# Silu moved to other units, and one 1024-element scan in place of two 512-element scans in 14 of 24 units of a Mamba kernel

## Chip, cores and metric

The kernel runs on one core of a Trainium2 chip. The metric is the device time of one execution in microseconds (us). The kernel before takes 11815.42 us, the median of 3 runs (11808.57 to 11817.72).

## What is computed

Two layers work on an image x of 2 x 96 x 128 x 128 (batch, channels, height, width). Layer 0 adds a four-direction Mamba block to x, then a feed-forward block in 8-bit floats; layer 1 adds a 3x3 convolution and a second feed-forward block. Each has a normalisation ahead of it. The change is inside the Mamba block. For each direction, with L = 16384 positions, 192 inner channels and 16 states:

```
xc = silu(conv1d(in-projection of x)); z = the other half of the projection
dt = softplus(dt_raw @ dt_w.T + dt_b)
dA[t] = exp(dt[t] * A)                      per channel and state
h[t]  = dA[t] * h[t-1] + dt[t] * B[t] * xc[t]
y[t]  = sum over states of h[t] * C[t]  +  D * xc[t]
out   = (y * silu(z)) @ outp_w.T
```

The recurrence in h is the part that can't be cut into independent pieces: it is a scan along t.

## The kernel before

For each of the two images the kernel normalises, runs the Mamba part, and then runs a fused stage of both feed-forward blocks and the convolution. The Mamba part takes the four directions in two pairs. A pair's 2 x 192 channels fill three groups (g = 0, 1, 2) of 128 partitions. A **step** is one block of T = 512 positions of one pair; there are 64 steps for an image and 128 in all. A **unit** is one group and two neighbouring states, so a step has 3 x 8 = 24 units, numbered u = 0 to 23 (k counts them across steps). For a unit:

- ACT (ScalarE) writes dA for both states to a PSUM tile `da` of 128 x 2 x 512 with two Exp instructions (`decay`, L364). The pool has three such tiles, and the loop asks for unit k+2 while unit k is scanned.
- POOL (GpSimd) multiplies the broadcast rows of B by dt*xc in place (`b_part`, L354), four states, that is two units, at a time, and adds the carried-in state to the first column of each state (L358), after one product for a group's start (L357). So a scan may start from 0.
- DVE (VectorE) runs the scan of each state (`scan`, L368), in place in `da`, and then multiplies both states by C (L456, in `behind`). In three units of a step (u = 4, 8, 10; the list BY_POOL) the scan writes into the B tile instead, and POOL does the product (L375).
- ACT copies the last column of h to `hst` (L457), and PE (TensorE) sums the products over states into one PSUM tile `y` (L372). At the end of a group DVE multiplies y by silu(z) (`gated`, L379).

Every engine's order is the order in which the Python code issues. [...] The main loop, for each k, issues this: the steps queued for (k, 0); the scan of the first state; `behind(k-1)`, that is the product, the copy to hst and the sums of the unit before; `decay(k+2)`; the scan of the second state; and the steps queued for (k, 1). On even k `b_part` of units k+2 and k+3 goes ahead of all that. On DVE, this puts the product of unit k-1 between the two scans of unit k.

While one step is scanned, the preparation of the next (or of the one after: its position list runs past 24 into the following step) is issued in small parts, from the list `at` in `prologue`: (position, 0 or 1 for the two places in a unit, function). ACT's parts are `conv_out` (L241), `gate_out` (L249), `rows_out` (L274), `dt_exp` (three instructions, L291 to L294), `dt_ln` (three, L299 to L302), `entry` (L320), `collect` (L393, L395), and `silu` (L261, L262): a load of another function table, one Silu over 128 x 1536, and the load of the usual table. POOL's parts are `dt_q` (L305), `dt_log` (L308), `dt_sum` (L311) and `dt_u` (L315). The small tiles e, q and ln between ACT and POOL have one buffer each, so ACT's `dt_exp` of one group waits for POOL's `dt_q` of the group before. PE's parts (`conv`, `gate`, `rows`, `dt_in`, `project`) all go through one PSUM bank, `misc`. SP issues the broadcasts of B and C rows from DRAM (`row_tile`, `fetch`), the re-sorting of xc and sz (`mix`), and the rows' way to DRAM.

Of the kernel before, what the change touches and what calls it, by code (L numbers as in the profile page):

```python
# [14 lines left out]
AF = mybir.ActivationFunctionType  # L15
ALU = mybir.AluOpType
# [17 lines left out]
C_AHEAD = 2  # L34
AHEAD = 2
BY_POOL = ((0, 8), (1, 0), (1, 4))
BCO = 32
NBC = 4 * S

# [2 lines left out]
def tile_metaformer(ctx: ExitStack, tc: tile.TileContext, a: dict, out: bass.AP):  # L42
    nc = tc.nc
# [5 lines left out]
    def const(name, shape):  # L49
        t = cpool.tile(list(shape), F32, name=name)  # L50
        nc.sync.dma_start(t, a[name])
        return t
# [7 lines left out]
    minus_one = cpool.tile([128, 1], F32, name="minus_one")  # L60
# [14 lines left out]
    convb = const("convb", (128, 2, NG))  # L75
    bcw = const("bcw", (128, 2, NG, BCO + NBC))
    dtw = const("dtw", (2 * RK, 2, NG * 128))
# [5 lines left out]
    amat = cpool.tile([128, 2, NG, S], F32, name="amat")  # L83
# [103 lines left out]
    def mamba(acc, xnr, xnc):  # L187

        with ExitStack() as st:
# [26 lines left out]
            def prologue(pi, i, d):  # L216

                rev = pi == 1
                lo = L - (i + 1) * T if rev else i * T
# [44 lines left out]
                def rows():  # L264

                    d["ps"] = misc()
                    for g in range(NG):
                        nc.tensor.matmul(  # L268
                            d["ps"][0 : BCO + NBC, :], bcw[:, pi, g, :], d["xc"][:, g, :], start=g == 0, stop=g == NG - 1
                        )  # L270

                def rows_out():
                    d["rows"] = one.tile([BCO + NBC, T], F32, name="rows")
                    nc.scalar.copy(d["rows"], d["ps"][0 : BCO + NBC, :])  # L274

                def rows_to_dram():

                    d["bcd"] = rows_d.tile([2, S // 4, 2, 4, T], F32, name="bcd")
                    nc.sync.dma_start(d["bcd"].rearrange("k q d s t -> (k q d s) t"), d["rows"][BCO:, :])

# [41 lines left out]


                first = pi == 0 and i == 0
                at = [(-3, 1, load), (3, 0, partial(mix, "xc")), (11, 0, partial(silu, "xc"))]
                at += [(9, 0, partial(mix, "sz")), (31, 1, partial(silu, "sz"))]
                at += [(12, 0, rows), (13, 1, rows_out), (14, 0, rows_to_dram)]
                for g, k in ((1, 1), (0, 5), (2, 9)):
                    at += [(k, 0, partial(conv, g)), (k + 1, 1, partial(conv_out, g))]
                for g, k in ((1, 7), (0, 17), (2, 21)):  # L330
                    at += [(k, 0, partial(gate, g)), (k + 1, 0, partial(gate_out, g))]
                dts = ((24, 25, 26, 27), (31, 32, 33, 35)) if first else ((18, 19, 20, 22), (22, 23, 24, 26))
                for g, ks in enumerate(((14, 15, 16, 18), *dts)):
                    at += [(k, 0, partial(f, g)) for k, f in zip(ks, (dt_in, dt_exp, dt_ln))]
                    at += [(ks[3] - 1, 1, partial(dt_q, g))]
                    at += [(ks[3] + m, 0, partial(f, g)) for m, f in ((1, dt_log), (1, dt_sum), (2, dt_u))]
                    if i > 0:
                        at += [((20, 24, 29)[g], 1, partial(entry, g))]

                outs = (conv_out, gate_out, rows_out, dt_exp)  # L340
                at = [(k, where, getattr(f, "func", f) not in outs, f) for k, where, f in at]
# [18 lines left out]
            def decay(pi, d, g, s):  # L360

                da = ps_w.tile([128, 2, T], F32, name="da")
                for j in range(2):
                    nc.scalar.activation(da[:, j, :], d["dt"][g], AF.Exp, scale=amat[:, pi, g, s + j : s + j + 1])  # L364
                return da

            def scan(j, da, b, h):
                nc.vector.tensor_tensor_scan(h[:, j, :], da[:, j, :], b[:, j, :], 0.0, ALU.mult, ALU.add)  # L368

            def sums(s, y, c):  # L370
                for j in range(2):
# [27 lines left out]
            units = [(g, s) for g in range(NG) for s in range(0, S, 2)]  # L399
            nu = len(units)  # L400
            total = nu * len(steps)
# [3 lines left out]
            def later(k, where, rank, f, *args):  # L405
                todo.setdefault((k, where), []).append((rank, partial(f, *args)))

            def issue(k, where):
                for _, f in sorted(todo.pop((k, where), ()), key=lambda p: p[0]):
                    f()  # L410

            for k, where, rank, f in prologue(*steps[0], state[0]):
                if k < nu:
                    f()
                else:
                    later(k - nu, where, rank, f)

            def prepare(n):
                if n < len(steps):
                    for m, where, rank, f in prologue(*steps[n], state[n]):  # L420
                        k = (n - 1) * nu + m
                        if k < 0:
                            f()
                        else:
                            later(k, where, rank, f)

            prepare(1)
            bs, cs, das, hs, quads = {}, {}, {}, {}, {}

            def fetch(k, n, ahead, m):  # L430
                if k < total:
                    t = row_tile(state[k // nu], *units[k % nu], n, ahead)
                    m[k], m[k + 1] = t[:, 0:2, :], t[:, 2:4, :]
                    if n == 0:
                        quads[k] = t

            def feed(k):

                if k < total:
                    n = k // nu  # L440
                    b_part(steps[n][1], state[n], *units[k % nu], quads.pop(k))

            def feed_decay(k):
                if k < total:
                    n = k // nu
                    das[k] = decay(steps[n][0], state[n], *units[k % nu])
# [3 lines left out]
            def behind(k):  # L450

                n, u = divmod(k, nu)
                (pi, i), d, (g, s) = steps[n], state[n], units[u]
                h, c = hs.pop(k), cs.pop(k)
                if (g, s) not in BY_POOL:
                    nc.vector.tensor_tensor(c, h, c, ALU.mult)  # L456
                nc.scalar.copy(hst[:, g, s : s + 2], h[:, :, T - 1])  # L457
                if s == 0:
                    if k > 0:
                        pn, pu = divmod(k - 1, nu)  # L460
                        gated(steps[pn][0], state[pn], units[pu][0], ys.pop(k - 1))
                    y = ps_y.tile([128, T], F32, name="y")
                    nc.tensor.matmul(y, dmat[:, pi, g, :], d["xc"][:, g, :], start=True, stop=False)  # L463
                else:
                    y = ys.pop(k - 1)
                ys[k] = y
                if (g, s) in BY_POOL:
                    later(k + 1, 1, True, by_pool, h, c)
                    later(k + 3, 1, True, sums, s, y, c)
                else:  # L470
                    sums(s, y, c)
                if k == total - 1:
                    gated(pi, d, g, y)
                if s == S - 2 and g > 0:
                    later(k + 4, 0, True, project, pi, i, d, g)
                    later(k + 5, 1, False, collect, pi, d, g)
# [7 lines left out]
            for k in range(total + 6):  # L484
                n, u = divmod(k, nu)
                if u == nu - 3:

                    prepare(n + 2)
                if k % 2 == 0:
                    fetch(k + 2 * B_AHEAD, 0, B_AHEAD, bs)  # L490
                    feed(k + AHEAD)
                issue(k, 0)
                if k < total:
                    (g, s) = units[u]
                    da, b = das.pop(k), bs.pop(k)
                    hs[k] = b if (g, s) in BY_POOL else da
                    scan(0, da, b, hs[k])
                if 0 < k <= total:
                    behind(k - 1)
                feed_decay(k + AHEAD)  # L500
                if k < total:
                    scan(1, da, b, hs[k])
                if k % 2 == 0:
                    fetch(k + 2 * C_AHEAD, 1, C_AHEAD, cs)
                issue(k, 1)
# [101 lines left out]
    for b in range(NB):  # L607
        xnr = dpool.tile([C, L], F32, name="xnr")
        xnc = dpool.tile([C, L], F32, name="xnc")
        normalize(b, acc, xnr, xnc)  # L610
        mamba(acc, xnr, xnc)
        ffn_and_conv(b, acc)


def _layout(v):
# [9 lines left out]
    xw = v["L0_conv_xproj_w"]  # L625
    bcw = np.zeros((2, 2 * DI, BCO + NBC), f)
    dtw = np.zeros((2 * RK, 2, 2 * DI), f)
# [56 lines left out]
```

## Time and profile before

| what | value |
|---|---|
| median of 3 runs | 11815.42 us |
| the profiled execution: its own time | 11813.3 us |
| its span | 11811.5 us |
| busy in the span: DVE | 10818.5 us, 92% |
| PE | 10510.1 us, 89% |
| POOL | 10203.6 us, 86% |
| ACT | 8548.6 us, 72% |
| granted TensorE clock | 0.99 |
| step of the Mamba part: nine Silu of `sz`, from 2927.8 to 3577.1 us, so 649.3 us for 8 steps | 81.16 us |

A span is cut into the 40 slices of the page's second part: the two Mamba parts take about 18 slices each, with the busy DVE, POOL and DMA; the slices with POOL at 1 are the fused stage. In the timeline an instruction's line gives its start, its duration, engine, source line and operation, then the number merged into the line (x2), and, in brackets, how long the engine stood idle ahead of it and what released it. Neighbours on one engine overlap a little: a scan lasts 1.21 us, but the next instruction starts 1.12 us after it did. For sums, the distance from start to start is therefore used, and it is called the pitch.

### The profile page before, as it was taken

The page shows a single profiled execution, that of the slowest core. Times are in us where ns is not written, and L with a number is a line of the kernel's source. Part 1 is how long each engine was busy: PE and PEld are TensorE (multiplying, and loading weights), DVE is VectorE, ACT ScalarE, POOL GpSimd, SP SyncE. Part 2 cuts the span into 40 slices and gives each one's busy share as a digit, 9 for nine tenths or more (in the row PEclk, how much of TensorE's full clock was granted, in tenths as well). Part 3 has the DMA queues.
Part 4 walks back from the last instruction along what each step waited for, and adds up shares of the span by engine and source line. Part 5 has one row for each costly group of instructions (what it writes and reads, how often), then busy time and mean ns, then how long its engine had stood idle before and what let it go on. Part 6 is the DMA issues. An engine that isn't in the chain of part 4 may idle for free. (4 is left out here: it accounts for less than half of the span.)

```text
span 11811.5 us, 96408 instructions
## 1 busy us (share of the span) xinstructions
PE 10510.1 (89%) x24208; PEld 3894.5 (33%) x24208; DVE 10818.5 (92%) x10512; ACT 8548.6 (72%) x15094; POOL 10203.6 (86%) x5468
## 2 busy tenths in 40 slices
PE   7888888989888889889978888888898898888899
PEld 2333333333333333333323333333333333333333
DVE  6999999999999999994469999999999999999944
ACT  6777777777777777775567777777777777777755
POOL 5999999999999999991159999999999999999911
PEclk9999999999999999999989999999999999999999
DMA  7888888888888888880068888888888888888800
GB/s 263 323 323 324 321 327 321 320 330 318 327 324 323 324 324 321 327 317 24 26 242 319 327 324 322 324 325 320 328 320 323 328 318 327 324 323 323 319 14 13
DMA packets 540774, 3417.11 MB, mean 289 GB/s; under 512 B 67532, under 2 KB 68652, under 8 KB 143832
## 3 DMA queue, kind: packets, MB, share of 16 engines
q1 hardware_dynamic: 539960, 3410.16, 75.6%
q8 instruction: 195, 3.19, 0.1%
q14 instruction: 363, 2.97, 0.1%
q0 software_dynamic: 256, 0.79, 0.0%
HBM read 3289.04 MB, written 54.53 MB: 283 GB/s over the span
## 5 line engine op out<-in xcount | busy, mean ns | idle before, releaser
L354 POOL TENSOR_TENSOR row<-dtu,row 128x2048 f32<-128x2048 f32 x1536 | 6957.6, 4530 | 11.4 <-DMA row<-bcd 8.7
L368 DVE TENSOR_TENSOR_SCAN da<-da,row 128x512 f32<-128x512 f32 x5376 | 6324.3, 1213 | 208.0 <-ACT da L364 127.7
L372 PE MATMUL y<-row,ident 128*128 128x512 f32 x12288 | 5778.2, 604 | 667.5 <-DVE row L456 643.5
L364 ACT ACTIVATE da<-dt,amat 128x512 f32<-128x512 f32 x6144 | 4249.0, 692 | 184.3 <-POOL dt L311 1.7
L372 PEld LDWEIGHTS y<-row,ident 128*128 128x128 f32 x12288 | 2231.1, 190 | 4058.8 <-issue 2155.2
L456 DVE TENSOR_TENSOR row<-da,row 128x1024 f32<-128x1024 f32 x2688 | 3233.6, 1203 | 0.1
L457 ACT COPY hst<-da 128x2 f32<-128x2 f32 x2688 | 423.6, 158 | 2400.8 <-DVE row L456 2380.7
L213 PE MATMUL misc<-xb,inx 96*64 96x512 f32 (+1 forms) x2048 | 956.5, 610 | 130.8 <-ACT hst L457 110.4
L579 POOL TENSOR_TENSOR acc<-acc,y 96x512 f32<-96x512 f32 x128 | 147.6, 1153 | 993.9 <-DVE y L578 993.9
L368 DVE TENSOR_TENSOR_SCAN row<-da,row 128x512 f32<-128x512 f32 x768 | 927.3, 1207 | 50.6 <-ACT da L364 44.8
L213 PE MATMUL misc<-xa,inx 96*64 96x512 f32 (+1 forms) x2048 | 940.8, 602 | 27.0 <-DMA xa<-xnr 17.3
L375 POOL TENSOR_TENSOR row<-row,row 128x1024 f32<-128x1024 f32 x384 | 904.0, 2354 | 18.0 <-DVE row L368 17.1
L305 POOL TENSOR_TENSOR q<-e,q 128x512 f32<-128x512 f32 x384 | 488.5, 1272 | 261.3 <-ACT hst L457 173.4
L591 PE MATMUL pc<-pad,kw 96*96 96x512 f32 x1152 | 567.0, 593 | 0.0
L463 PE MATMUL y<-xc,dmat 128*128 128x512 f32 x768 | 421.3, 630 | 149.9 <-DVE sz L379 149.9
L311 POOL TENSOR_TENSOR dt<-dt,ln 128x512 f32<-128x512 f32 x384 | 488.6, 1272 | 30.1
L213 PEld LDWEIGHTS misc<-xa,inx 96*64 96x64 f32 (+1 forms) x2048 | 314.5, 163 | 604.2 <-issue 426.0
L315 POOL TENSOR_TENSOR dtu<-dt,xc 128x512 f32<-128x512 f32 x384 | 488.6, 1272 | 0.5
L308 POOL TENSOR_TENSOR ln<-ln,q 128x512 f32<-128x512 f32 x384 | 487.5, 1270 | 0.2
L389 PE MATMUL misc<-sz,gmat 128*96 128x512 f32 x1024 | 483.6, 594 | 0.0
L268 PE MATMUL misc<-xc,bcw 128*96 128x512 f32 x768 | 364.4, 611 | 117.6 <-ACT xc L261 91.9
L213 PEld LDWEIGHTS misc<-xb,inx 96*64 96x64 f32 (+1 forms) x2048 | 316.9, 164 | 434.1 <-issue 204.0
(82 smaller groups left out, 8926.2 us busy)
## 6 DMA issues: line engine op xcount, KB each, us to landing
row<-bcd SPq DMA_DIRECT2D x3072, 1024.0 KB, 6.4
xc<-mix SPq DMA_DIRECT2D x256, 128.0 KB, 5.4
sz<-mix SPq DMA_DIRECT2D x256, 128.0 KB, 8.4
xa<-xnr SPq DMA_DIRECT2D x124, 193.1 KB, 5.2
xb<-xnc SPq DMA_DIRECT2D x124, 193.1 KB, 5.4
bcd<-rows SPq DMA_DIRECT2D x128, 128.0 KB, 6.9
acc<-in_x_dram SPq DMA_DIRECT2D x16, 768.0 KB, 5.9
xnr<-xn SPq DMA_DIRECT2D x16, 768.0 KB, 4.3
```

The costliest lines, as they stand in the source:

```text
L213: nc.tensor.matmul(ps[rows, :], w(PAIRS[pi][d], k, lo, hi), src[d][:, k : k + T], **se)
L305: nc.gpsimd.tensor_tensor(d["q"], d["e", g], d["q"], ALU.subtract)
L308: nc.gpsimd.tensor_tensor(d["ln"], d["ln"], d["q"], ALU.add)
L311: nc.gpsimd.tensor_tensor(d["dt"][g], d["dt"][g], d["ln"], ALU.add)
L315: nc.gpsimd.tensor_tensor(dtu, d["dt"][g], d["xc"][:, g, :], ALU.mult)
L354: nc.gpsimd.tensor_tensor(b, d["dtu"][g][:, None, :].broadcast_to((128, 4, T)), b, ALU.mult)
L364: nc.scalar.activation(da[:, j, :], d["dt"][g], AF.Exp, scale=amat[:, pi, g, s + j : s + j + 1])
L368: nc.vector.tensor_tensor_scan(h[:, j, :], da[:, j, :], b[:, j, :], 0.0, ALU.mult, ALU.add)
L372: nc.tensor.matmul(y, ident, c[:, j, :], start=False, stop=s + j == S - 1)
L375: nc.gpsimd.tensor_tensor(c, h, c, ALU.mult)
L456: nc.vector.tensor_tensor(c, h, c, ALU.mult)
L591: nc.tensor.matmul(pc, kw[:, t, :], rows, start=t == 0, stop=t == 8)
```

## The change

```diff
+SPLIT = (4, 5, 10, 11, 15, 16, 18, 19, 22, 23)
...
-                at = [(-3, 1, load), (3, 0, partial(mix, "xc")), (11, 0, partial(silu, "xc"))]
-                at += [(9, 0, partial(mix, "sz")), (31, 1, partial(silu, "sz"))]
-                at += [(12, 0, rows), (13, 1, rows_out), (14, 0, rows_to_dram)]
+                at = [(-3, 1, load), (3, 0, partial(mix, "xc")), (11, 1, partial(silu, "xc"))]
+                at += [(9, 0, partial(mix, "sz")), (29, 1, partial(silu, "sz"))]
+                at += [(13, 0, rows), (14, 1, rows_out), (15, 0, rows_to_dram)]
...
-                dts = ((24, 25, 26, 27), (31, 32, 33, 35)) if first else ((18, 19, 20, 22), (22, 23, 24, 26))
-                for g, ks in enumerate(((14, 15, 16, 18), *dts)):
+                dts = ((24, 25, 26, 27), (32, 33, 34, 35)) if first else ((18, 19, 20, 22), (22, 23, 24, 26))
+                for g, ks in enumerate(((15, 16, 17, 18), *dts)):
                     at += [(k, 0, partial(f, g)) for k, f in zip(ks, (dt_in, dt_exp, dt_ln))]
-                    at += [(ks[3] - 1, 1, partial(dt_q, g))]
+                    at += [(ks[3], 1, partial(dt_q, g))]
                     at += [(ks[3] + m, 0, partial(f, g)) for m, f in ((1, dt_log), (1, dt_sum), (2, dt_u))]
...
                 da = ps_w.tile([128, 2, T], F32, name="da")
+                part = units.index((g, s)) not in SPLIT
+                if part:
+                    nc.scalar.activation(da[:, 1, 0:1], minus_one, AF.Copy, scale=0.0)
                 for j in range(2):
-                    nc.scalar.activation(da[:, j, :], d["dt"][g], AF.Exp, scale=amat[:, pi, g, s + j : s + j + 1])
+                    lo = j if part else 0
+                    scale = amat[:, pi, g, s + j : s + j + 1]
+                    nc.scalar.activation(da[:, j, lo:], d["dt"][g][:, lo:], AF.Exp, scale=scale)
                 return da

             def scan(j, da, b, h):
-                nc.vector.tensor_tensor_scan(h[:, j, :], da[:, j, :], b[:, j, :], 0.0, ALU.mult, ALU.add)
+                da, b, h = (t[:, j, :] if j is not None else t.rearrange("p j t -> p (j t)") for t in (da, b, h))
+                nc.vector.tensor_tensor_scan(h, da, b, 0.0, ALU.mult, ALU.add)
...
-                    scan(0, da, b, hs[k])
+                    scan(0 if u in SPLIT else None, da, b, hs[k])
                 if 0 < k <= total:
                     behind(k - 1)
                 feed_decay(k + AHEAD)
-                if k < total:
+                if k < total and u in SPLIT:
                     scan(1, da, b, hs[k])
```

In 14 units of a step, called joined units below, one scan runs over both states' 1024 elements. The zero that ACT writes at the first column of the second state's dA cuts the chain there: 0 * h + b is b, which holds the carried-in state. The Exp of the second state then covers 511 elements. The joined scan stands where the first scan stood, and the product of the unit before comes after it instead of between two scans. The 10 units of SPLIT keep their two scans.

The Silu of xc goes from (11, 0) to (11, 1), behind `decay(13)`. The Silu of sz goes from (31, 1) to (29, 1), that is from u = 7 to u = 5 of the following step, ahead of `entry` of group 2. The rows' product, copy and store move one unit later, as do `dt_in`, `dt_exp` and `dt_ln` of group 0. For every group POOL's `dt_q` moves from the end of one unit to the end of the next, so that the `b_part` of two units, which stood between `dt_q` and `dt_log`, now comes ahead of both.

## Prediction

> **What bounds the kernel now.** I read four views in this order: busy time by engine, with one stretch inside the Mamba part; the groups of instructions; who waited for whom; then the timeline of one step, engine by engine. First the busy times, and the stretch from 2000 to 3000 us (columns: its length, then PE, PEld, DVE, ACT, POOL, clock, DMA share, GB/s):
>
> ```profile
> PE 10510.1 (89%) x24208; PEld 3894.5 (33%) x24208; DVE 10818.5 (92%) x10512; ACT 8548.6 (72%) x15094; POOL 10203.6 (86%) x5468
> ```
>
> ```profile
> 2000.00:3000.00 1000.00, 894.99 (x2049) 330.02 (x2048) 981.77 (x888) 748.71 (x1327) 965.61 (x508) 1.00 0.85 323
> ```
>
> In the Mamba part DVE is busy 98% and POOL 97%: two engines near their limit. Who waits, with total and number of times:
>
> ```profile
> POOL q L305 <- ACT hst L457: 173.4, 126, 3.0
> DVE da L368 <- ACT da L364: 127.7, 126, 1.0
> DVE row L368 <- ACT da L364: 44.8, 112, 0.4
> ```
>
> DVE stalls only behind ACT, twice a step (172.5 us in all); it never waits for POOL in the steady state. POOL waits once a step, 1.38 us, at the first `dt_q`. So DVE with its two stalls sets the step of 81.16 us, and POOL follows with 1.4 us to spare. The stalls, on DVE and on ACT:
>
> ```profile
> 3012.17 1.22 DVE L368 TENSOR_TENSOR_SCAN da<-da,row 128x512 f32<-128x512 f32 x1
> 3013.80 1.22 DVE L368 TENSOR_TENSOR_SCAN row<-da,row 128x512 f32<-128x512 f32 x1 [0.41 <-ACT da L364]
> ...
> 3021.81 1.22 DVE L368 TENSOR_TENSOR_SCAN da<-da,row 128x512 f32<-128x512 f32 x1
> 3024.03 1.23 DVE L368 TENSOR_TENSOR_SCAN da<-da,row 128x512 f32<-128x512 f32 x1 [1.01 <-ACT da L364]
> 3043.72 2.33 DVE L368 TENSOR_TENSOR_SCAN da<-da,row 128x512 f32<-128x512 f32 x2
> 3045.96 1.20 DVE L456 TENSOR_TENSOR row<-da,row 128x1024 f32<-128x1024 f32 x1
> ```
>
> ```profile
> 3018.40 1.28 ACT L261 ACT_TABLE_LOAD   x1
> 3019.70 1.48 ACT L261 ACTIVATE xc<-xc 128x1536 f32<-128x1536 f32 x1
> 3021.20 1.28 ACT L262 ACT_TABLE_LOAD   x1
> 3022.49 0.19 ACT L457 COPY hst<-row 128x2 f32<-128x2 f32 x1
> 3022.59 1.41 ACT L364 ACTIVATE da<-dt,amat 128x512 f32<-128x512 f32 x2
> ```
>
> Each stall ends with the second Exp behind a Silu burst (3018.40 to 3022.49: 4.09 us). The last two DVE lines give pitches: two scans 2.24, so 1.12 each; a product also 1.12; the gated product (3039.76 to 3040.35) 0.59. A step's DVE work is 48 x 1.12 + 21 x 1.12 + 3 x 0.59 = 79.05, plus 0.13 at each of three places where both scans of a unit stand together (3.49 for three scans, where 3.36 would do): 79.4. With the stalls and 0.1 of lost overlap at each, 79.4 + 1.62 = 81.1, against 81.16 measured.
>
> POOL's pitches:
>
> ```profile
> 3035.17 0.20 POOL L358 TENSOR_TENSOR row<-row,enter 128x4 f32<-128x4 f32 x1
> 3036.80 1.28 POOL L305 TENSOR_TENSOR q<-e,q 128x512 f32<-128x512 f32 x1 [1.42 <-ACT hst L457]
> 3038.02 4.53 POOL L354 TENSOR_TENSOR row<-dtu,row 128x2048 f32<-128x2048 f32 x1
> 3042.63 0.20 POOL L358 TENSOR_TENSOR row<-row,enter 128x4 f32<-128x4 f32 x1
> 3042.78 1.27 POOL L308 TENSOR_TENSOR ln<-ln,q 128x512 f32<-128x512 f32 x1
> 3044.13 1.27 POOL L311 TENSOR_TENSOR dt<-dt,ln 128x512 f32<-128x512 f32 x1
> 3045.36 4.54 POOL L354 TENSOR_TENSOR row<-dtu,row 128x2048 f32<-128x2048 f32 x1
> ```
>
> A quad with its edge takes 4.76 (3038.02 to 3042.78), 4.95 with L357, L375 2.31. A 512-element operation takes 1.23 if the next needs nothing of it, 1.35 if the next reads its result (ln to dt). Sum: 9 x 4.76 + 3 x 4.95 + 3 x 2.31 + 3 x (1.23 + 1.35 + 1.23 + 1.24) = 79.77; with the wait of 1.4 it is 81.17.
>
> [...]
>
> **The change, part by part.**
>
> *The joined scan.* From gated (512: 0.59) and product (1024: 1.12), the fixed part of an instruction is 0.06; the scan then streams 512 in 1.06. A scan of 1024 has pitch 2 x 1.06 + 0.06 = 2.18 to 2.19, and saves about 0.055. No row shows one: below, nothing excludes 2.13 (no fixed part at all)[...]. I take 2.185. DVE per step: 20 x 1.12 + 14 x 2.185 + 21 x 1.12 + 1.77 + 0.26 (the joined unit 9 drops one of the three places) = 78.54. This is 0.9 less than 79.4.
>
> *ACT's extra copy.* Between 0.09 (overlapped) and 0.29 (the 128x16 ACTIVATE L320); I take 0.2. It lengthens each joined unit's turn on ACT (hst, copy, two Exps) from 1.55 to 1.75, and 1.81 to the end of the second Exp.
>
> *Slack.* The Exps of unit k+2 may start once the product of k-1 has ended. Before, they end 2.8 us ahead of their scan (3045.4 against 3048.2). In joined rows, with the product behind the long scan, they start 3.4 us after the start of unit k and have to be done at 6.6: 6.6 - 3.4 - 1.8 = 1.4 left. The dt work fits: in units 16 to 24 ACT carries 1.82 (`dt_exp`) or 1.93 (`dt_ln`) beside 1.6 to 1.75 in a unit of 3.3 to 3.9, and a backlog of 0.1 to 0.4 never reaches 1.4.
>
> *Silu of sz.* Time 0 is the start of unit 4. DVE: unit 5 at 3.36, unit 6 at 5.73 (two scans, no product: unit 4's is POOL's), unit 7 at 9.04, unit 8 at 12.35; product 5 ends at 9.12. ACT: hst and Exps for unit 6 from 2.35 to 4.10; collect 1.05, to 5.15; hst and Exps for 7 (no product to wait for) 1.6, to 6.75; Silu to 10.84; `entry` 0.29, to 11.1; hst and Exps for 8 end at 12.93. Unit 8 starts 0.6 late, 0.7 with the overlap.
>
> *Silu of xc.* Time 0 is unit 10. Exps for 12 end at 4.10, `conv_out` at 4.77, Exps for 13 at 6.37, Silu at 10.46, Exps for 14 at 12.27; unit 14 starts at 12.35. No stall. Its two users follow: the rows, now at unit 13, and `dt_in` at 15 keep their one-unit distances. So DVE and ACT alone would give 78.54 + 0.7 = 79.25, and DVE would no longer be last.
>
> *POOL.* What is late next is POOL. Its wait of 1.4 goes, but `dt_log` now reads q directly behind `dt_q` (1.35 instead of 1.23, three times), and for one group `b_part` directly follows the `dt_u` that it reads (once more): 79.77 + 4 x 0.12 = 80.25. This is its floor with no wait. The bounds are 79.77 (the waits cost nothing) and 80.25 plus whatever makes it wait. With POOL last, the first `dt_q` comes behind one more quad (4.73) while ACT's `dt_ln` comes one unit (3.3) later, so the wait is covered by 1.4. The tightest of its other waits, the product of unit 10, has about 0.7 to spare.
>
> *Queues.* rows to DRAM move from 14 to 15; the first fetch that reads them is issued at 18, three units or 10 us later; the store lands in 6.9 us. The cover is 3 us here, and a further four units until `b_part` uses the rows. PE's 72.6 us a step stay. The first step's shifted `dt` costs nothing that repeats.
>
> *Sum.* 81.16 to 80.25 is 0.91 a step; over 126 steps in the steady state, 115 us. Against the profiled execution's 11813.3 (span 11811.5 plus 1.8) this is 11698; the median, 2 us higher, gives 11700.
>
> **Rivals.**
>
> 1. *POOL bound at 80.25* (forecast): 11700. For it: 97% busy, contiguous but for one wait. Against: only 0.9 us above DVE's own sum. Spread 11670 to 11725.
> 2. *The added POOL waits cost nothing*, or overlap as before: floor 79.77, 1.39 x 126 = 175, 11640 (11615 to 11665).
> 3. *ACT is tied to POOL*: `dt_exp` of group 2 waits for `dt_q` of group 1 (e has one buffer), which moved a unit later. On POOL it ends 49.6 us after the quad of unit 8; ACT wants it at 50.3. With POOL late by 1 us, ACT takes this over, and with 2.9 more DVE does. A mixed cycle of about 80.75: 0.41 x 126 = 52, 11763 (11735 to 11790).
> 4. *Slower: PE late ahead of the Silu bursts.* `collect` and `conv_out` stand directly ahead of Silu on ACT and wait for PE, 89% busy. [...] each us of delay there reaches units 8 and 14 in full, since the slack is gone. Against: now such waits are short (ACT waited 21.1 us on `conv_out` in all). It decides from 81.3 - 79.25 = 2.1 us a step. With 1.25 us at each place, 81.75: +74, 11890.
> 5. *No effect*: joined scans cost as much as two, and POOL keeps waiting elsewhere: 11815.
>
> **How the numbers follow.** Chances: forecast 0.58, second 0.14, third 0.14, slower 0.10, none 0.04. 0.2% (24 us) is about what a measurement of this kernel can tell from no change. Faster by more than that: 0.58 + 0.14 + 0.11 of the third = 0.83, rounded to 0.82; within: 0.03 + 0.04 = 0.07; slower 0.11. The range 11625 to 11780 holds the forecast, most of the second and most of the third, 0.58 + 0.12 + 0.11 = 0.81.
>
> **What would show it.** A 1024-element scan with a pitch near 2.19; a 128x1 ACT copy near 0.2; the wait POOL q <- ACT gone; DVE waiting for POOL's rows (L354, L358) about 1 us a step, mostly at units 8, 12 and 14, and for ACT at unit 8 at most; POOL near 98% in the Mamba part; a step of 80.25. The prediction is wrong if POOL still waits, if the scan's pitch is above 2.24, or if ACT's waits on PE ahead of Silu grow.

## The result, and the profile after

The changed kernel takes 12003.11 us (median of 4 runs, 11998.69 to 12006.19) against 11812.17 for the kernel before in the same comparison: a ratio of 1.0161, 95% interval 1.0143 to 1.0179. It is slower, where a gain of 1% was forecast. In the profiled execution the span is 12004.4 us, and a step, from the Silu of xc at 2908.6 us to the eighth after it at 3571.0, is 662.4 / 8 = 82.80 us instead of 81.16.

First the busy times by engine, then a stretch of 1000 us in the Mamba part (columns as before: length, PE, PEld, DVE, ACT, POOL, clock, DMA share, GB/s):

```profile
PE 10618.6 (88%) x24208; PEld 3978.5 (33%) x24208; DVE 10738.7 (89%) x8720; ACT 8845.1 (74%) x16886; POOL 10219.6 (85%) x5468
```

```profile
2000.00:3000.00 1000.00, 891.68 (x1998) 334.06 (x1997) 951.56 (x698) 759.82 (x1463) 944.18 (x492) 0.97 0.83 316
```

DVE has fallen from 98% to 95%, but POOL, which was to go to 98%, is at 94%. Neither of the two is the limit all the time: each waits for a chain that contains the other. Who waited for whom (total, times, longest):

```profile
POOL row L355 <- DMA row<-bcd: 290.3, 119, 6.1
ACT e L292 <- POOL q L306: 282.4, 165, 3.3
DVE da L378 <- POOL row L359: 224.6, 247, 2.2
DVE row L378 <- POOL row L359: 217.0, 124, 1.8
```

DVE now waits for POOL, as forecast, but 3.5 us a step (441.6 in all) and not about 1. POOL's wait at q is gone: 1.1 us where 173.4 were. In its place POOL waits 290 us, 2.3 a step, for B rows to arrive from DRAM, where the kernel before lost 8.7 us in all. Here is POOL's timeline around one such wait, which is for the rows of units 20 and 21:

```profile
3002.13 4.52 POOL L355 TENSOR_TENSOR row<-dtu,row 128x2048 f32<-128x2048 f32 x1
3006.72 0.21 POOL L359 TENSOR_TENSOR row<-row,enter 128x4 f32<-128x4 f32 x1
3010.97 4.53 POOL L355 TENSOR_TENSOR row<-dtu,row 128x2048 f32<-128x2048 f32 x1 [4.04 <-DMA row<-bcd]
3015.57 0.20 POOL L359 TENSOR_TENSOR row<-row,enter 128x4 f32<-128x4 f32 x1
3015.72 1.28 POOL L306 TENSOR_TENSOR q<-e,q 128x512 f32<-128x512 f32 x1
3017.08 1.27 POOL L309 TENSOR_TENSOR ln<-ln,q 128x512 f32<-128x512 f32 x1
```

The same moment in SP's queue (start, duration, number of fetches), and on PE:

```profile
2991.61 1.23 SPq L351 DMA_DIRECT2D row<-bcd  x2
3003.43 0.80 SPq L351 DMA_DIRECT2D row<-bcd  x2
3005.14 0.32 SPq L351 DMA_DIRECT2D row<-bcd  x1
```

```profile
2993.71 3.48 PE L382 MATMUL y<-row,ident 128*128 128x512 f32 x4 [2.13 <-DVE row L466]
2996.98 2.98 PE L269 MATMUL misc<-xc,bcw 128*96 128x512 f32 x6
2999.80 5.31 PE L382 MATMUL y<-row,ident 128*128 128x512 f32 x12
```

SP issues fetches strictly in turn: B of 16, C of 14, B of 18, C of 16, B of 20, C of 18. From 2992.8 to 3003.43, for 10.6 us, it issues none. The first of the two fetches at 3003.43 is that of C rows for units 16 and 17. It needs the buffer of units 10 and 11, and unit 10 is one of POOL's: its sums on PE are issued three units later, at the end of unit 13. On PE these are the second four matmuls of the line at 2999.80 (four make a unit of two states: the page counts 12288 on this line for 3072 units), so they end near 3003.4, and SP moves at once. The B rows of unit 20 stood behind in the queue. Their own buffer had been free for 7 us (its last scan, unit 13's, ended at 2995.9), and they land 7 us after they are issued, when POOL has been idle for 4. A part of the delay is PE's speed: the line at 2993.71 took 3.48 us for four matmuls, where 1.88 is usual (the last section comes back to this).

The same place in the kernel before, PE and SP:

```profile
3023.89 1.88 PE L372 MATMUL y<-row,ident 128*128 128x512 f32 x4
3026.44 3.70 PE L372 MATMUL y<-row,ident 128*128 128x512 f32 x8 [0.67 <-DVE row L456]
```

```profile
3030.17 0.80 SPq L350 DMA_DIRECT2D row<-bcd  x2
```

There too SP stood in C rows until unit 10's sums ended at 3030.1. But that was 6.1 us after the start of unit 13 (3024.03), and after the change it is 9.9 (3003.43 against 2993.57). And there POOL waited at q for ACT in the meantime, did q, and came to those rows at 3038.02, when they had landed. The trace of before hardly shows a wait for DMA (8.7 us), because another wait lay over it; run 15 tests this.

### The profile page after: what moved, and what is told of

It is laid out like the page before. It is cut to its first block, busy times and chain, and to the rows that moved or that the text cites. A ratio compares the mean times of both kernels' runs of the same rounds, so it can differ in the third digit from the quotient of the medians.

```text
span 12004.4 us, 96788 instructions
## 1 busy us (share of the span) xinstructions
PE 10618.6 (88%) x24208; PEld 3978.5 (33%) x24208; DVE 10738.7 (89%) x8720; ACT 8845.1 (74%) x16886; POOL 10219.6 (85%) x5468
## 3 DMA queue, kind: packets, MB, share of 16 engines
q1 hardware_dynamic: 539960, 3410.16, 74.4%
## 5 line engine op out<-in xcount | busy, mean ns | idle before, releaser
L382 PE MATMUL y<-row,ident 128*128 128x512 f32 x12288 | 5908.1, 617 | 822.2 <-DVE row L466 820.2
L378 DVE TENSOR_TENSOR_SCAN da<-da,row 128x512 f32<-128x512 f32 (+1 forms) x3712 | 6209.3, 1695 | 333.2 <-POOL row L359 224.6
L372 ACT ACTIVATE da<-dt,amat 128x512 f32<-128x512 f32 (+1 forms) x6144 | 4247.7, 691 | 192.9 <-POOL dt L312 1.6
L378 DVE TENSOR_TENSOR_SCAN row<-da,row 128x512 f32<-128x512 f32 (+1 forms) x640 | 913.3, 1427 | 222.4 <-POOL row L359 217.0
L214 PE MATMUL misc<-xa,inx 96*64 96x512 f32 (+1 forms) x2048 | 970.8, 617 | 28.1 <-DMA xa<-xnr 17.6
L214 PE MATMUL misc<-xb,inx 96*64 96x512 f32 (+1 forms) x2048 | 974.4, 620 | 18.7 <-ACT mix L250 13.5
L292 ACT ACTIVATE e<-misc,dtb 128x512 f32<-128x512 f32 x384 | 262.2, 683 | 407.5 <-POOL q L306 282.4
L214 PEld LDWEIGHTS misc<-xa,inx 96*64 96x64 f32 (+1 forms) x2048 | 332.8, 168 | 643.7 <-issue 490.3
L287 PE MATMUL misc<-rows,dtw 12*128 12x512 f32 x768 | 439.2, 651 | 11.1 <-ACT sz L250 9.4
```

The source lines that it names most:

```text
L214: nc.tensor.matmul(ps[rows, :], w(PAIRS[pi][d], k, lo, hi), src[d][:, k : k + T], **se)
L372: nc.scalar.activation(da[:, j, lo:], d["dt"][g][:, lo:], AF.Exp, scale=scale)
L378: nc.vector.tensor_tensor_scan(h, da, b, 0.0, ALU.mult, ALU.add)
L382: nc.tensor.matmul(y, ident, c[:, j, :], start=False, stop=s + j == S - 1)
```

## The experiments

Each run is compared with the kernel before, measured beside it (medians of 11809.48 to 11813.75 us). Ratios carry their 95% intervals; "step" is the mean distance of seven or eight Silu of xc near 3000 us.

**1. One more buffer for C rows.**

```diff
-                t = gen.tile([128, 4, T], F32, name=f"row{k}", bufs=ahead + 1)
+                t = gen.tile([128, 4, T], F32, name=f"row{k}", bufs=ahead + 1 + k)
```

(Also `io` with 1 buffer and dt, dtu with 3, for the space.)

> Theory (the queue): in the changed kernel POOL is last, as forecast at 80.25 us a step, but loses a further 2.3 us because SP, which issues all row fetches in order, stands in a fetch of C rows until PE has done the sums of unit 10, and the B rows of unit 20 are queued behind it. A fourth buffer for C rows takes that wait away: POOL's wait for B rows falls from 290 us to under 60, the step to about 80.4, the time to 11720 (11690 to 11760). Rival (the transfers): the rows come late because the DMA engines are short of throughput (median landing 7.1 us against 6.4); then nothing is gained, 11950 to 12010. Two other pools are made smaller to hold the buffer (xa and xb single, three buffers for dt and dtu); each theory expects nothing of that.

Measured: 11840.81 us, 1.0026 (1.0016 to 1.0037). POOL's wait for B rows is 6.4 us in all. So the queue is shown, and throughput is refuted: nothing was taken off the DMA engines, whose main queue moved 3410.16 MB in both kernels. But the time stayed 120 us above the expectation. Two waits that were small in the changed kernel (7.6 and 1.1 us) have come up:

```profile
DVE sz L389 <- PE y L382: 203.7, 128, 3.1
POOL q L306 <- ACT hst L467: 138.2, 90, 3.1
```

**2. B rows first.**

```diff
                 if k % 2 == 0:
                     fetch(k + 2 * B_AHEAD, 0, B_AHEAD, bs)
+                    if k > 0:
+                        fetch(k + 2 * C_AHEAD - 2, 1, C_AHEAD, cs)
...
-                if k % 2 == 0:
-                    fetch(k + 2 * C_AHEAD, 1, C_AHEAD, cs)
```

> The changed kernel with each fetch of C rows issued two units later, behind the fetch of B rows of that moment, and no other edit. Theory (the queue): SP no longer holds B rows back; POOL's wait for B rows nearly goes, 11700 to 11780, unless the C rows now come late for the product (a wait of DVE L466 on a DMA would show it). Rival (the transfers): about 12000, with the wait unchanged.

Measured: 11839.81 us, 1.0025 (1.0015 to 1.0035). POOL's wait for B rows is gone, so this agrees with the first run by another way. C rows come late by 4.7 us in all for DVE's products and by 26.1 for POOL's. The same wait on PE appears: once a step, 1.4 to 1.6 us, ahead of the gated product of unit 9. The timelines of PE, ACT and DVE in this run show its cause:

```profile
3013.34 0.64 PE L214 MATMUL misc<-xa,inz 96*64 96x512 f32 x1 [0.78 <-ACT hst L467]
...
3014.34 5.42 PE L382 MATMUL y<-row,ident 128*128 128x512 f32 x12
```

```profile
3009.38 1.28 ACT L263 ACT_TABLE_LOAD   x1
...
3012.61 0.67 ACT L242 ACTIVATE xc<-misc,convb 128x512 f32<-128x512 f32 x1
```

```profile
3019.80 0.69 DVE L389 TENSOR_TENSOR sz<-y,sz 128x512 f32<-128x512 f32 x1 [1.38 <-PE y L382]
```

The z projection of group 1 (L214, inz) may start on PE only when ACT has copied the projection before it out of the one `misc` tile (the copy runs from 3012.61 to 3013.28, and PE starts at 3013.34), and that copy now stands behind the Silu of sz, which the change moved from unit 7 to unit 5. The sums of units 6, 4 and 7 stand behind the projection on PE (x12), and the gated product waits for the last of them. The page names `hst` as what released PE; hst follows the copy directly, and hst is nothing that the projection needs.

**3. The moves without joined scans** (`SPLIT = tuple(range(24))`).

> All moved steps of the change, but two scans in every unit, as before. Theory (the queue): the product of a unit ends 1.1 us earlier in its unit than in a joined one, so the C buffers come free earlier, but the rows' matmuls still stand ahead of the sums on PE: POOL's wait for B rows between 0.5 and 1.5 us a step, POOL at 80.25 besides, 11760 to 11890. If the joined scans were the whole loss: about 11700. If the moves were the whole loss: 12000.

Measured: 11965.53 us, 1.0130 (1.0115 to 1.0145), a step of 82.21. POOL waits 222.4 us for B rows. This is above the expected range: the moves alone bring four fifths of the loss (1.30 of 1.61%).

**4. Joined scans without the moves.**

```diff
-[(11, 1, partial(silu, "xc"))], (29, 1, silu sz), rows 13, (14, 1), 15; dt of group 0 (15, 16, 17, 18); dt_q at (ks[3], 1)
+[(11, 0, partial(silu, "xc"))], (31, 1, silu sz), rows 12, (13, 1), 14; dt of group 0 (14, 15, 16, 18); dt_q at (ks[3] - 1, 1)
```

> Joined scans in the same 14 units, with every step of the preparation where it stood before the change. Theory (the queue): POOL's floor is 79.77; its wait for B rows is small, since the rows' matmuls stay a unit earlier; but the Silu bursts now stand ahead of Exps with 1.4 us less slack, so DVE waits for ACT 2 to 3.5 us a step in place of 1.4: a step of 81 to 82.5, 11790 to 11980. If the joined scans alone make the loss through the C rows, POOL waits for DMA here too and it is about 12000.

Measured: 12011.14 us, 1.0170 (1.0155 to 1.0185), a step of 82.83. Slightly above the expected range, and the loss is another one: B rows cost 15.4 us only, DVE waits 217.8 us for ACT (172.5 before), POOL 381.4 us at q (173.4 before) and then DVE 206 us for POOL. The two halves of the change each lose about what the whole does; the losses don't add, and don't come by the same path.

**5. POOL's units summed one unit sooner.** The changed kernel with one edit:

```diff
-                    later(k + 3, 1, True, sums, s, y, c)
+                    later(k + 2, 1, True, sums, s, y, c)
```

> The changed kernel with one edit: PE's sums of the three units whose product POOL makes are issued one unit sooner (unit 10's at the end of unit 12, so ahead of the rows' matmuls that the change moved to unit 13). Theory: those sums hold the C buffer that SP waits for, and for unit 4 they stand ahead of unit 7's sums that the gated product of unit 9 waits for. POOL's wait for B rows falls from 290 us to under 120 and the time to 11720 to 11830. Rival (PE is short of time altogether, at 0.96 of its clock): the waits only change places, 11900 to 12000.

Measured: 11693.62 us, 0.9901 (0.9886 to 0.9916), a step of 643.0 / 8 = 80.38. The waits of this run:

```profile
POOL row L355 <- DMA row<-bcd: 13.3, 27, 1.2
DVE sz L389 <- PE y L382: 43.2, 80, 2.1
POOL q L306 <- ACT hst L467: 7.1, 17, 0.6
```

One number undoes the loss and brings what was forecast for the change, 11700. PE has the same work and the same mean granted clock (0.971 against 0.973), so the order of its work decides. That its speed adds nothing to the loss doesn't follow (last section).

**6. The projection behind the sums.** To run 2:

```diff
-                    at += [(k, 0, partial(gate, g)), (k + 1, 0, partial(gate_out, g))]
+                    at += [(k, int(g == 1), partial(gate, g)), (k + 1, int(g == 1), partial(gate_out, g))]
```

> B rows first (as in the run before) and the z projection of group 1 issued behind the sums of its unit, its copy behind the Exps of the next. Theory: DVE's wait of 200 us on PE ahead of the gated product comes from that projection, which stands ahead of three units' sums and waits on ACT for the copy that the earlier Silu of sz holds back. The wait falls under 80 us, POOL's wait at q under 60 us, and the time to 11700 to 11790. Rival (PE too slow): the wait stays, 11840.

Measured: 11713.89 us, 0.9918 (0.9903 to 0.9933). DVE's wait ahead of the gated product falls from 200.4 to 76.8 us, POOL's at q from 133.9 to 36.0. The second chain is shown, by an edit of its own.

**7. B rows first, and sums sooner** (edits of 2 and 5).

> B rows first, and POOL's units summed one unit sooner. Theory: both queues are freed; the step comes to POOL's floor of 80.25 and 0.2 to 0.5 of rest: 11710 to 11770. Rival (PE too slow): 11840 as without the sums' edit.

Measured: 11673.00 us, 0.9883 (0.9869 to 0.9898), a step of 642.0 / 8 = 80.25. A stretch of it:

```profile
2000.00:3000.00 1000.00, 914.10 (x2074) 345.44 (x2073) 984.44 (x725) 791.60 (x1519) 979.79 (x511) 0.98 0.86 328
```

POOL is at 98%, and the step is the forecast floor. The time is some 40 us below the expected range; the step in this stretch, taken for all, would give 11695, so some 20 us come from elsewhere.

**8. As 7, with dt_q one unit sooner** (`(ks[3] - 1, 1, partial(dt_q, g))`).

> As the run before, with POOL's dt_q one unit sooner again, where it stood before the change (a quad between it and dt_log). If POOL's floor rules, its four added waits on itself go, 80.25 to 79.77: 60 us less than the run before, 11650 to 11710. If POOL now waits for ACT at q as it did before the change (1.4 us a step), the gain is nothing or less: 11710 to 11820.

Measured: 12090.24 us, 1.0238 (1.0220 to 1.0255), worse than either expectation. ACT's `dt_ln` of group 0 stays a unit later than before the change, so POOL waits at q 570 us in all (88 of them belong to the two starts), nearly all of it at group 0, and DVE waits 490 us for POOL. With `dt_ln` moved, `dt_q` can't go back alone.

**9. The kernel before with the sums sooner.**

> The kernel before, with only the sums of POOL's units one unit sooner. Theory: nothing there waits for those sums (POOL lost 8.7 us in all to B rows, DVE 25 us to PE ahead of the gated product), so 11790 to 11815. Rival (the sums are worth more by themselves, and what the last runs gained was not given back by the change): under 11760.

Measured: 11803.21 us, 0.9991 (0.9983 to 1.0000), a step of 81.16 as before. Worth nothing by itself there: DVE and its two Silu stalls set that step. What the edit gains in run 5 it gains from the change's loss.

**10. Moves and sums, two scans in every unit.**

> The change's moves with the sums one unit sooner, and two scans in every unit. If POOL's floor of 80.25 rules, DVE at 79.4 and no Silu stall left is hidden under it, and the joined scans bring next to nothing: within 25 us of the 11694 of the changed kernel with the sums sooner. If the joined scans' 0.9 us a step count, 11760 to 11810.

Measured: 11670.05 us, 0.9879 (0.9863 to 0.9896), a step of 560.6 / 7 = 80.09. As fast as run 7 without one joined scan, and 24 us faster than run 5, the same kernel with them, which is within the 25 us expected. DVE no longer waits for ACT (0.6 us in all against 172.5), so the moved Silu bursts do their work; POOL's floor sets the step, and what DVE would save with joined scans is hidden below it.

**11. Only unit 10's sums sooner** (`k + (2 if u == 10 else 3)`).

> The changed kernel with only unit 10's sums one unit sooner; units 4 and 8 as in the change. Theory: this frees SP, so POOL's wait for B rows falls under 100 us; DVE still waits 150 to 200 us on PE ahead of the gated product of unit 9, since unit 4's sums stay ahead of unit 7's: 11780 to 11850, like the run with a C buffer more. If 11690 to 11720, unit 4's sums did not matter.

Measured: 11842.15 us, 1.0024 (1.0016 to 1.0032). POOL's wait for B rows is 89.5 us, DVE still waits 154.3 us ahead of the gated product: as expected. Unit 10's sums hold SP; the edit for the two other units is worth the remaining 149 us of run 5. There the wait ahead of the gated product fell to 43.2, and the rest of the wait for B rows to 13.3.

**12. The Silu of xc and the rows where they were.** (silu (11, 0), rows 12, (13, 1), 14; the rest as changed.)

> The changed kernel with the Silu of xc and the rows' product, copy and store where they stood before. Theory: with the rows' matmuls a unit sooner the sums of units 10 and 12 are not behind them, and POOL's wait for B rows falls from 290 to under 100 us; but the Silu of xc again stands ahead of unit 13's Exps, with the smaller slack of a joined unit: DVE waits for ACT 2 us a step there, 11880 to 12000. If the joined product alone holds the C rows, POOL's wait for B rows stays above 200 us.

Measured: 12169.60 us, 1.0303 (1.0288 to 1.0319). Both expectations failed: the time is 170 us above the range, and POOL's wait for B rows went up, to 503.8 us. DVE's wait for ACT came much as expected (203 us), nearly all of it at unit 13. In the timeline unit 12's product, which follows unit 13's scan, is late by that, and so are unit 12's sums, unit 10's behind them, and the B rows. This run can't tell whose lateness counts, so the next two take one cause each.

**15. The kernel before with only dt_q one unit later** (`(ks[3], 1, partial(dt_q, g))`).

> The kernel before with only POOL's dt_q one unit later, as in the change. Theory: before, POOL stood at q 1.4 us a step while the B rows of unit 20 landed; now it comes to those rows 2.6 us sooner and waits for them instead: POOL's wait at q (173 us) goes and its wait for B rows rises from 9 us to 60 to 200 us; DVE still sets the step, 11800 to 11850. Rival (the rows land early enough by themselves): no wait for rows, 11800 to 11815.

Measured: 11888.75 us, 1.0067 (1.0052 to 1.0082). The waits of this run:

```profile
POOL row L354 <- DMA row<-bcd: 129.1, 79, 3.3
POOL row L354 <- DVE da L368: 82.6, 52, 3.2
POOL q L305 <- ACT hst L457: 0.9, 2, 0.5
DVE row L368 <- POOL row L358: 134.4, 124, 1.6
```

POOL's wait at q turned into a wait for the rows, and q's own work now comes after the rows instead of ahead of them. It cost even more than expected: DVE waits for POOL 1.1 us a step. This one move, with nothing joined and nothing moved on ACT or PE, brings 79 us.

**16. Shorter rows' product.** The contributions of two of the three groups are left out.

```diff
-                    for g in range(NG):
-                        nc.tensor.matmul(... bcw[:, pi, g, :], d["xc"][:, g, :], start=g == 0, stop=g == NG - 1)
+                    g = 0
+                    nc.tensor.matmul(... bcw[:, pi, g, :], d["xc"][:, g, :], start=True, stop=True)
```

> The changed kernel with the rows' product over one of the three groups only (the contributions of two groups to B, C and dt_raw are left out), so that PE has 1.9 us less to do at the place to which the change moved it, ahead of the sums of units 12 and 10. Theory: POOL's wait for B rows falls from 290 us to between 30 and 150, and the step by as much: 11800 to 11900. Rival (the later product of joined units alone makes the C rows late): above 230 us, 11980 to 12005.

Measured: 11897.91 us, 1.0076 (1.0059 to 1.0093); POOL's wait for B rows 211.9 us. The time is in the expected range and the wait is not: it fell only by 78 us. With about 1.9 us of PE work gone at that place (four of the six matmuls of the line at 2996.98), the loss falls from 1.61 to 0.76%. The rows' matmuls are a part of the lateness, not the whole.

**13 and 14. Two units for POOL instead of three**, with joined scans and without (`BY_POOL = ((0, 8), (1, 4))`, on run 7; in 14 also `SPLIT = tuple(range(24))`).

> B rows first and sums sooner, joined scans, and unit 8's product given from POOL to DVE (two POOL units a step in place of three). POOL's floor goes from 80.25 to 77.9, DVE's sum from 78.5 to 79.66. Theory (the joined scans save 0.6 to 0.7 a step, hidden so far under POOL's floor): a step of 79.8 to 80.1, 11600 to 11660, and 60 to 110 us less than the next run, which has two scans in every unit. Rival (the saving is eaten by ACT's waits in joined units): both alike.

> The run before with two scans in every unit. DVE's sum is 79.4 + 1.12 - 0.13 = 80.4, POOL's floor 77.9: DVE alone sets the step, 80.4 to 80.6, 11690 to 11740.

Measured: 11768.86 us (0.9964, 0.9951 to 0.9977) with joined scans, 11725.12 us (0.9929, 0.9914 to 0.9943) without. The time without joined scans is in its expected range, and the gain that was expected of them did not come. With POOL relieved, DVE's sum with joined scans is 0.7 us a step lower (79.66 against 80.4), and still the kernel is 44 us slower. Without them DVE hardly waits; with them it waits for POOL (88.5 us at L359), POOL at q (178.6 us, against 66.8) and ACT for PE (181.1 us, against 68.4).

## Why the prediction was wrong, step by step

- *POOL's floor: right, but the changed kernel does not reach it.* Run 7, with the queues freed, has a step of 80.25, the floor that was summed from the pitches, and run 10 one of 80.09, so the sum was at least 0.16 high. The changed kernel itself stands at 82.80. The surcharge for a POOL instruction that reads its predecessor's result is there (3015.72 to 3017.08: 1.36, where 1.23 was measured before if the next needs nothing of it).
- *Operations: right.* The joined scan and the zero's copy on DVE and ACT:

```profile
3021.30 2.29 DVE L378 TENSOR_TENSOR_SCAN da<-da,row 128x1024 f32<-128x1024 f32 x1
3023.50 1.21 DVE L466 TENSOR_TENSOR row<-da,row 128x1024 f32<-128x1024 f32 x1
```

```profile
3013.82 0.17 ACT L368 ACTIVATE da<-minus_one 128x1 f32<-128x1 f32 x1
3014.03 1.41 ACT L372 ACTIVATE da<-dt,amat 128x512 f32<-128x512 f32 x2
```

  The scan's pitch is 2.20, against 2.185 in the sum; the copy takes 0.174 on average with a pitch of 0.21, against the author's estimate of 0.2.
- *ACT's slack: right in effect.* DVE waits for ACT about 23 us in all at joined scans. The stall of 0.7 a step at unit 8 does not show, because DVE waits for POOL at units 6 and 8 instead; in run 7, where those waits are small, it is 52.6 us in all, 0.4 a step.
- *"Queues" is the step that failed.* It asked of SP only when the rows' store and the first fetch behind it are issued. It did not ask what SP's own fetches wait for, and what stands behind them, so this wait entered the sum at nothing; it measured 290 us, 2.3 a step. A C fetch waits for PE's sums, the late ones of POOL's units above all, and B fetches stand behind it. The sums are delayed by the rows' matmuls, which the change puts ahead of them (run 16); that the later product of joined units delays them too is read from the timelines, and no run takes it alone. The one wait that the step did sum was also too small: the store was to have 3 us of cover, but SP stands 401.4 us in all for it, 0.8 before. POOL loses little by that, since nearly all its wait for rows is at unit 20's, which are issued ahead of the store.
- *"The wait is covered by 1.4" was true and beside the point.* POOL no longer waits at q. But that wait and q's work had covered the landing of unit 20's rows. I gave the stall's end as a gain and named the next bound (POOL's work) without asking what POOL would arrive at sooner. Run 15 shows that this alone costs 79 us, on the kernel before.
- *"PE's 72.6 us a step stay" hid the second chain.* The work stays, but the copy behind the Silu of sz holds `misc`, the projection holds PE, and the gated product of unit 9 waits: 200 us in run 2, with the first chain gone. In the changed kernel itself this wait is 7.6 us; it lies behind the first.
- *Rivals.* The third is in the trace, 282 us of ACT at q, but reaches DVE little, and in runs 1, 2 and 5 it is gone (1.0 to 5.9 us in run 1 and 5) though dt_q stands at its moved place: so it follows from POOL's late rows. The fourth named PE's delay ahead of the Silu bursts. PE was the engine, but mostly by its order; the way led over SP and over `y`, not over ACT, whose wait on `conv_out` stayed (20.2 us after 21.1).
- *The joined scans' gain* is hidden below POOL's floor as forecast (run 10). That they lose when POOL is relieved (runs 13, 14) was not forecast. The cause is open. The product of unit k-1 comes about 1.1 us later in a joined unit (behind a scan of 2.20 in place of one of 1.12), and PE's sums and ACT's Exps start from it, but no run gave back only that; PE also has twice as many stretches at half clock in run 13 as in run 14 (192 and 97, last section).

How the 191 us split between the two chains, and within the first between dt_q, the rows' matmuls and the joined product, can't be given as a sum. The pieces overlap: 79 us for dt_q alone and 155 for all moves, each on the kernel before, and, against the changed kernel, 105 given back by shorter rows, 163 by B rows first, 310 by the sums sooner.

## What to carry to other kernels

SP's queue, which issues its transfers in turn, had a critical path of its own here: one C fetch held up the B rows behind it, and POOL waited 290 us for them. For every buffer that a transfer refills, ask which engine's instruction frees it, where that instruction stands in that engine's order, and which other transfer stands behind the fetch. When a wait is taken away, ask what the engine will reach sooner, and whether the old wait covered a landing there. With two engines near the limit, DVE at 98% and POOL at 97%, the saving of one was worth only what the other left (run 10, with two scans in every unit, is as fast as run 7 with joined ones), and an edit to the order of a third, one unit for a few sums on PE, was worth more than either: 310 us on the changed kernel (run 5).

## What was not expected of the hardware

The granted TensorE clock is lower with joined scans: 0.973 with the change, 0.961, 0.962 and 0.971 in runs 1, 2 and 5, against 0.99 before, 0.984 and 0.982 in the runs with all moves and no joined scan (3, 10); the pair 13 and 14, with the same PE work, has 0.966 and 0.979. The mean of a sums' matmul rose from 604 to 617 ns with the change.

The mean hides a pattern. In the clock records of the kernels before and after every entry is 1.0 or 0.5 of the full clock. The kernel before has 21 stretches at half clock (239 us in all), the changed kernel 146 (653 us), 131 of them 3.4 us long. In the first Mamba part (560 to 5300 us) there are 3 before and 62 after. PE's pauses of more than 1.5 us rose there from 3 to 161, and within the 4 us ahead of each of the 62 stretches such a pause begins. One stretch lies in the lines above: behind PE's pause of 2.13 us the mean clock from 2993.71 to 2997.00 is 0.55, and this is where four sums took 3.48 us. That the pauses bring the half clock is inferred from these records and not shown: no run changes the pauses alone.

These stretches go with a longer wait. In 36 of the 128 steps of the changed kernel PE has more than 1 us of half clock in the stretch from 19 to 7.5 us ahead of unit 20's `b_part`. In these steps POOL stands idle ahead of that `b_part` for 3.8 us on average, in the others for 2.2 (341 us in all; the profile puts some 50 of them down to DVE and not to the rows). The difference, 1.6 x 36 = 58 us, is an estimate of what half clock adds. In run 5, 64 steps have such a stretch, and POOL waits less than 0.1 us on average in either kind. So PE's speed seems to cost time only where the order leaves none between the sums and the rows.
